# A decoder layer's feed-forward: first product as one plain product with resident weights, in place of seven half-size products with streamed sums

## The chip, the cores and the metric

The kernel runs on one core of a Trainium2 chip. The metric is the device time of one execution in microseconds (us); lower is better. Engines are named as in the profile: PE is TensorE, DVE is VectorE, ACT is ScalarE, POOL is GpSimd, SP is SyncE, which only issues transfers here.

## What is computed

One post-norm decoder layer on x of shape (8, 512, 512) in float32: relative-position self-attention, cross-attention to a context (8, 512, 1024), and a feed-forward block, each followed by a residual sum and a layer norm. The change is in the feed-forward block alone, cut here to what matters:

```python
h = jax.nn.relu(jnp.einsum('bsd,hd->bsh', x, w1) + b1)   # w1: (2048, 512)
hq = float_quantize(h, 4, 3)
out = jnp.einsum('bsh,dh->bsd', hq, wq) + bq             # wq = quantized w2
x = _layernorm(x + float_quantize(out, 5, 10))
```

## The kernel before

There are two phases. The first (lines 190 to 618) computes self-attention for all rows and projects the context to keys and values; it keeps both in DRAM. It ends at about 1,000 us of the profiled span. The change does not touch its source.

The second phase (from line 631) goes over eight blocks t of 512 rows. In stage t the kernel does the attention of block t (`scores`, `attend`) and, woven between these steps, the dense work of the blocks before it: the output projection of block t-1 (`project_x1`, `project_u`), its norm (`normalize_x2`), the transposed reload of the result (`load_x2T`, `turn_x2`), the queries of block t+1 (`load_x1T`, `turn_x1`, `queries`), the hidden layer of block t-1, and `finish` of block t-2, which is the second feed-forward product in FP8, the residual and the last norm.

The order of PE, DVE, ACT and SP is written by hand. `dense` is a list of steps with a cost each, `attention` a second list; `weave` (line 1174) takes from the one or the other by these costs. `run` (line 676) adds 0.7 of a step's cost to a credit, and pays from it small pieces of DVE and ACT work that wait in the queues `side` and `urgent` (softmax pieces, norms, stores). So a step's cost sets the order in which instructions stand, and nothing else. Each engine then runs its own instructions in that order and waits on semaphores.

The hidden layer (line 991, `hidden_steps`) multiplies w1 (2048 x 512) by the block transposed, `x2T` (512 x 512). It splits both in two halves each way and uses seven products of half size in place of eight (the Winograd form of Strassen's scheme). Each of eight rounds n makes hidden rows n and n+8 (of 16 chunks of 128) from fourteen matmuls, each 128x128 by 128x256. Each float32 matmul stands as two instructions in the profile, so a round is 28 rows of 128x256. The seven left operands, four of them sums of w1's blocks, stand in a ring of three slots (`ring`). In stage t=1, POOL builds them (`load_w1`, `sums_of_a`) from w1 as it arrives in 128 KB pieces, and SP stores each slot to DRAM (`w1d`); in all later stages ACT's queue reloads a slot for each round, 896 KB each. The right operands are four quarters of `x2T` and three sums of them, built by DVE after the turn (`sums_of_x2`, line 742). Partial results go from PSUM through ACT copies and DVE adds (lines 1015, 1021, 1035, 1041, 1045, 1054) to the ReLU on ACT (line 1048), which writes `hq` in FP8. All of it shares four PSUM banks (`bank`, line 649) with the other dense steps.

In the last stretch, after block 7's attention, nothing is left to weave; there the code cuts `finish` of block 6, rows 2 and 3, into quarters, and places one in each round.

Two further places matter. Line 727 turns a block of 512 x 512 on DVE in four instructions after a transposed load. Line 857 moves each head pair's attention weights between partitions (`pT<-pb`, sixteen SP transfers of 128 KB) before `attend` can use them.

Of the kernel before, what the change touches and what calls it, by code (L numbers as in the profile page):

```python
# [13 lines left out]
ALU = mybir.AluOpType  # L14
# [28 lines left out]
def decoder_layer(  # L43
# [46 lines left out]
    w1d = [dram.tile([P, 7, 2, P], F32, name=f"w1d{n}") for n in range(HC // 2)]  # L90
# [540 lines left out]
    with ExitStack() as ph:  # L631
# [110 lines left out]
        def sums_of_x2(t):  # L742
            b = [
                x2T[t][:, 2 * i : 2 * i + 2, k * W : (k + 1) * W]
                for i in range(2)
                for k in range(2)
            ]
            sums_of_b(nc.vector, *b, *(tx[:, i] for i in range(3)))

        def turn_x2(t):  # L750
            for c in range(EC):
                turn_in_place(x2T[t], c)
            sums_of_x2(t)
# [202 lines left out]

        W = S // 2
        HH2 = HC // 2
        RING = 3

        def turn_last_x2(j):
            t = T - 1
            if j == 0:
                settle(("x2", t))
                x2T[t] = qx.tile([P, EC, S], F32, tag="x2T", name=f"x2T{t}")  # L970
            turn(x2T[t], x1[t], j, f"x2tr{t}")
            if j == NJ - 1:
                sums_of_x2(t)

        def load_w1(m):

            n = m % HH2
            w = ring[:, m % RING]
            if m >= HH2:
                nc.scalar.dma_start(w, w1d[n])  # L980
                return
            lo, hi = slice(n * P, (n + 1) * P), slice((n + HH2) * P, (n + HH2 + 1) * P)
            w1c = chunked(w1T)
            nc.sync.dma_start(w[:, A11], w1c[:, 0:2, lo])
            nc.sync.dma_start(w[:, A12], w1c[:, 2:4, lo])
            nc.sync.dma_start(w[:, S3], w1c[:, 0:2, hi])
            nc.sync.dma_start(w[:, A22], w1c[:, 2:4, hi])
            sums_of_a(nc.gpsimd, w)
            later.append([3, lambda: nc.sync.dma_start(w1d[n], w)])

        def hidden_steps(t):


            x, y, z, tm2 = {}, {}, {}, {}

            def product(ps, n, a, b, start):


                for e in range(2):
                    nc.tensor.matmul(  # L1000
                        ps[:, 0:W],
                        lhsT=ring[:, (t * HH2 + n) % RING, a, e, :],
                        rhs=b[:, e, :],
                        start=start and e == 0,
                        stop=e == 1,
                        skip_group_check=not start,
                    )

            def b(i, k):
                return x2T[t][:, 2 * i : 2 * i + 2, k * W : (k + 1) * W]  # L1010

            def p2(n):
                y[n] = bank(f"hy{t}_{n}")
                product(y[n], n, A12, b(1, 0), True)
                nc.scalar.copy(tmp[:, n % 2, 0:W], y[n][:, 0:W])

            def p5(n):
                z[n] = bank(f"hz{t}_{n}")
                product(z[n], n, S1, tx[:, 0], True)
                tm2[n] = sm.tile([P, W], F32, tag="tm2", bufs=2, name=f"tm2_{t}_{n}")  # L1020
                nc.scalar.copy(tm2[n], z[n][:, 0:W])

            def begin():

                tag, bufs = ("qT", 2) if t == T - 1 else ("hq", 1)
                hq[t] = qx.tile([P, HC, S], F8, tag=tag, bufs=bufs, name=f"hq{t}")
                p5(0)
                p2(0)

            def p13(n):  # L1030
                x[n] = bank(f"hx{t}_{n}")
                product(x[n], n, A11, b(0, 0), True)
                product(z[n], n, S4, b(1, 1), False)
                c11 = tmp[:, n % 2, 0:W]
                nc.vector.tensor_tensor(c11, x[n][:, 0:W], c11, ALU.add)  # L1035

            def p6(n):
                if t * HH2 + n + 2 < T * HH2:
                    load_w1(t * HH2 + n + 2)
                product(x[n], n, S2, tx[:, 1], False)  # L1040
                nc.scalar.copy(tmp[:, n % 2, W:S], x[n][:, 0:W])  # L1041
                if n + 1 < HH2:
                    p2(n + 1)
                c12 = tmp[:, n % 2, W:S]
                nc.vector.tensor_tensor(c12, z[n][:, 0:W], c12, ALU.add)

            def relu(n, qs, src):
                nc.scalar.activation(
                    hq[t][:, n, qs], src, AF.Relu, bias=col(C_B1 + n), saturate=False
                )  # L1050

            def p7(n):
                product(x[n], n, S3, b(0, 1), False)
                nc.vector.tensor_tensor(tm2[n], x[n][:, 0:W], tm2[n], ALU.add)  # L1054
                if n + 1 < HH2:
                    p5(n + 1)
                relu(n, slice(0, S), tmp[:, n % 2])

            def p4(n):
                product(x[n], n, A22, tx[:, 2], False)  # L1060
                relu(n + HH2, slice(0, W), x[n][:, 0:W])
                relu(n + HH2, slice(W, S), tm2[n])

            steps = of(1.7, begin)
            for n in range(HH2):
                steps += of(1.7, p13, n) + of(1.7, p6, n) + of(1.7, p7, n)
                steps += [(0.9, True, lambda n=n: p4(n))]
            return steps

        def finish(t, j, n, part=0, parts=1, block=None):  # L1070

            if j % n == 0 and part == 0:
                mvc[t] = sm.tile([P, n, 2], F32, tag="mv", name=f"mvc{t}_{j}")
            if part == 0:
                o_bank[j] = block or bank(f"o{t}_{j}")
            po = o_bank[j]
            for c in range(HC * part // parts, HC * (part + 1) // parts):
# [7 lines left out]
            if part < parts - 1:  # L1085
                return
# [22 lines left out]
        o_bank = {}  # L1109
# [36 lines left out]
        ring = tx = tmp = None  # L1146

        def take_ring():

            nonlocal ring, tx, tmp  # L1150
            ffn = big.tile([P, FC * 2 * E], F32, tag="big", name="ffn")
            at = 0

            def part(*shape):
                nonlocal at
                n = math.prod(shape)
                names = "abcd"[: len(shape)]
                w = ffn[:, at : at + n].rearrange(
                    f"p ({' '.join(names)}) -> p {' '.join(names)}",
                    **dict(zip(names, shape)),  # L1160
                )
                at += n
                return w

            ring = part(RING, 7, 2, P)
            tx = part(3, 2, W)
            tmp = part(2, S)
            load_w1(0)
            load_w1(1)

        def of(cost, f, *a):
            return [(cost, False, lambda: f(*a))]

        def weave(dense, attention):

            dense, attention = list(dense), list(attention)
            left = sum(c for c, _, _ in dense)  # L1180
            weights = sum(w for _, _, _, w in attention)
            nd, gap = 0, 2.0
            while dense or attention:
                ready = attention and (not dense or attention[0][1] <= nd)
                if ready and (not dense or gap <= 0.0 or (dense[0][1] and gap < 1.5)):
# [3 lines left out]
                else:  # L1189
                    cost, _, step = dense.pop(0)  # L1190
# [31 lines left out]
        def output_of(t):  # L1222
# [3 lines left out]
            for j in range(NJ - 1):  # L1226
                steps += of(2.7, project_x1, t, j)
            steps += of(3.8, attend_next, t, EC - 1)
            for j in range(NJ - 1):
                steps += of(2.7, project_u, t, j)  # L1230
            last = NJ - 1
            return steps + of(2.7, project_x1, t, last) + of(2.7, project_u, t, last)

        ET = mybir.EngineType
        with tc.manual_schedule(engines={ET.PE, ET.DVE, ET.Activation, ET.SP}):
# [11 lines left out]
            for t in range(T):  # L1247
# [3 lines left out]
                asked = [of(3.5, queries, t + 1, o, mq) for o in range(EC) if t + 1 < T]  # L1251
                asked = sum(asked, [])
                if t == 0:
# [25 lines left out]
                    for piece in pieces[:-2]:  # L1279
                        dense += of(6.9, piece)  # L1280
# [12 lines left out]
                else:  # L1293
                    done = [of(3.5, finish, t - 2, j, NJ) for j in range(NJ) if t > 1]
                    if t == 1:

                        done = [of(6.9, pieces[-2]), of(6.9, pieces[-1]), [], []]
# [7 lines left out]
                    if t == 1:  # L1305
                        dense += of(0.0, take_ring)
                    dense += done[2] + done[3]
                    if t + 1 < T:
                        dense += of(0.0, turn_x1, t + 1)
                    dense += asked[:2] + of(0.0, turn_x2, t - 1) + asked[2:]  # L1310
                    queried = len(dense)
                    hidden = hidden_steps(t - 1)
                    hidden[HC:HC] = of(0.0, load_x1, t)
                    dense += hidden
                weave(dense, attention_of(t, projected, queried))

            last = of(3.5, finish, T - 2, 0, NJ) + output_of(T - 1)
            last += of(0.0, normalize_x2, T - 1)
            last += of(3.5, finish, T - 2, 1, NJ)
            for j in range(NJ):  # L1320
                last += of(0.6, turn_last_x2, j)

            gaps = []
            for j in (2, 3):

                def quarter(j, i):
                    block = ps_s.tile([P, 2, S], F32, tag="s", name=f"ol{j}")[
                        :, 0
# [102 lines left out]
```

## Time and profile before

| What | Value |
|---|---|
| Median of 3 runs | 2190.15 us (2187.91 to 2191.26) |
| The profiled execution's own time | 2196.65 us |
| Its span (first to last instruction) | 2194.5 us |
| Mean granted PE clock | 0.978 of full |
| PE busy | 2055.4 us, 94% of the span |
| DVE busy | 1567.5 us, 71% |
| ACT busy | 553.3 us, 25% |
| POOL busy | 170.7 us, 8% |
| Bytes moved by DMA | 316.35 MB, mean 144 GB/s |

A matmul row shows a busy time with a modelled end: one 128x512 float32 row reads 592 ns, but the next one starts 429 ns after it. So the rate of a stream is read from the starts of neighbouring rows, and a busy share of 94% still hides small waits. In the rows of the view in order of time, the bracket at the end tells how long the engine sat idle before the row, and what released it.

### The profile page before, as it was taken

The page shows a single profiled execution, that of the slowest core. Times are in us where ns is not written, and L with a number is a line of the kernel's source. Part 1 is how long each engine was busy: PE and PEld are TensorE (multiplying, and loading weights), DVE is VectorE, ACT ScalarE, POOL GpSimd, SP SyncE. Part 2 cuts the span into 40 slices and gives each one's busy share as a digit, 9 for nine tenths or more (in the row PEclk, how much of TensorE's full clock was granted, in tenths as well). Part 3 has the DMA queues.
Part 4 walks back from the last instruction along what each step waited for, and adds up shares of the span by engine and source line. Part 5 has one row for each costly group of instructions (what it writes and reads, how often), then busy time and mean ns, then how long its engine had stood idle before and what let it go on. Part 6 is the DMA issues. An engine that isn't in the chain of part 4 may idle for free.

```text
span 2194.5 us, 21443 instructions
## 1 busy us (share of the span) xinstructions
PE 2055.4 (94%) x7312; PEld 1186.9 (54%) x7312; DVE 1567.5 (71%) x2602; ACT 553.3 (25%) x1267; POOL 170.7 (8%) x156
## 2 busy tenths in 40 slices
PE   7999999999989999988997999999999999998898
PEld 5564665466447576733344446365464553644555
DVE  3799998999989998255664586665856767657434
ACT  2011101110201111122233335243352332524322
POOL 1000110011001001100013101001000010100000
PEclk9999999999999999999998999999999999999999
DMA  8130443035124235884486777676675757656612
GB/s 291 58 130 10 144 168 125 17 129 179 55 96 135 77 111 174 273 230 124 104 176 187 176 152 218 110 202 160 133 225 114 175 170 136 204 125 156 180 51 89
DMA packets 269117, 316.35 MB, mean 144 GB/s; under 512 B 142929, under 2 KB 171601, under 8 KB 269009
## 3 DMA queue, kind: packets, MB, share of 16 engines
q1 hardware_dynamic: 244720, 234.99, 41.4%
q10 hardware_dynamic: 24288, 80.00, 11.2%
q8 instruction: 58, 0.95, 0.2%
q14 instruction: 51, 0.41, 0.1%
HBM read 181.22 MB, written 66.58 MB: 113 GB/s over the span
## 4 chain that ended last, share of the span: by engine, by line
PE 58%; DVE 26%; DMA 8%; SPq 3%; issue 2%; ACT 2%; POOL 0%; ACTq 0%; DVEq 0%; POOLq 0%
PE hx L1000 9%; PE px L540 7%; PE pox L925 5%; PE pox L913 5%; PE hz L1000 4%; PE s L792 4%; PE pz L540 4%; DVE pv L429 4%; PE av L891 4%; PE ps_q L339 3%; DVE pb L844 2%; PE po L455 2%; SPq L857 2%; PE hy L1000 2%; DVE pv L439 2%
## 5 line engine op out<-in xcount | busy, mean ns | idle before, releaser
L817 ACT ACTIVATE pe<-pe,nmax 128x512 f32<-128x512 f32 x256 | 182.2, 713 | 245.6 <-DVE nmax L807 243.7
L807 DVE CUSTOM_DVE_ANT_0 pe<-s,mb 128x512 f32<-128x512 f32 x256 | 164.2, 682 | 56.0 <-PE s L792 54.8
L844 DVE STREAM_TRANSPOSE pb<-pe 128x512 f32<-128x512 f32 x256 | 161.0, 680 | 0.7 <-issue 0.2
L429 DVE TENSOR_TENSOR pv<-v,sc 128x2048 f32<-128x2048 f32 x64 | 148.5, 2321 | 2.0
L380 DVE TENSOR_TENSOR pq<-qw,k 128x2048 f32<-128x2048 f32 x64 | 147.2, 2300 | 1.1
L1000 PE MATMUL hx<-ffn 128*128 128x256 f32 x512 | 134.9, 386 | 13.2 <-DVE ffn L1035 6.6
L389 DVE TENSOR_REDUCE sc<-pq 128x64 f32<-128x2048 f32 x64 | 146.1, 2282 | 1.4
L1000 PE MATMUL hx<-x2T,ffn 128*128 128x256 f32 x512 | 138.2, 393 | 8.9 <-ACT ffn L1041 5.0
L891 PE MATMUL av<-pT,vx 128*64 128x512 f32 x512 | 124.8, 632 | 14.3 <-DMA pT<-pb 14.3
L772 PE MATMUL psq<-x1Ts,w_tgt 128*128 128x512 f32 x256 | 122.0, 632 | 16.5 <-DVE x1Ts L727 16.5
L832 DVE TENSOR_SCALAR pe<-pe,rden 128x512 f32<-128x512 f32 x256 | 132.6, 560 | 4.5
L792 PE MATMUL s<-kT,qTx 64*128 64x512 f32 x512 | 128.2, 617 | 3.4 <-DVE nmax L807 3.2
L1000 PEld LDWEIGHTS hx<-x2T,ffn 128*128 128x128 f32 x512 | 94.8, 192 | 52.3 <-issue 27.9
L455 PE MATMUL po<-w_o,aoT 128*128 128x512 f32 x256 | 117.1, 600 | 0.7 <-ACT aoT L452 0.7
L339 PE MATMUL ps_q<-w_in,xt 128*128 128x512 f32 x256 | 116.8, 594 | 0.3 <-DVE qw L366 0.3
L925 PE MATMUL pox<-w_xo,uT 128*128 128x512 f32 x256 | 115.2, 598 | 0.0
L1000 PEld LDWEIGHTS hx<-ffn 128*128 128x128 f32 x512 | 91.5, 190 | 42.5 <-DVE tm L1054 11.8
L913 PE MATMUL pox<-w_xo,x1Ts 128*128 128x512 f32 x256 | 114.4, 595 | 0.0
L339 PE MATMUL ps_k<-w_in,xt 128*128 128x512 f32 x256 | 114.0, 593 | 0.0
L932 DVE TENSOR_TENSOR x<-pox,x 128x512 f32<-128x512 f32 x32 | 22.1, 692 | 126.7 <-PE pox L925 79.2
L339 PE MATMUL ps_v<-w_in,xt 128*128 128x512 f32 x256 | 111.6, 594 | 0.0
L1078 PE MATMUL o<-w2q,hq 128*128 128x512 fp8e4 x480 | 106.1, 379 | 0.0
(179 smaller groups left out, 3114.6 us busy)
## 6 DMA issues: line engine op xcount, KB each, us to landing
pT<-pb SPq DMA_DIRECT2D x512, 128.0 KB, 2.4
ffn<-w1d ACTq DMA_DIRECT2D x56, 896.0 KB, 6.3
ch<-in_ctxT_dram SPq DMA_DIRECT2D x56, 256.0 KB, 3.3
td<-tx SPq DMA_DIRECT2D x28, 384.0 KB, 3.2
tx<-td SPq DMA_DIRECT2D x28, 384.0 KB, 5.6
r<-in_x_dram SPq DMA_DIRECT2D x32, 256.0 KB, 3.7
xt<-in_xT_dram SPq DMA_DIRECT2D x32, 256.0 KB, 2.6
x1d<-r ACTq DMA_DIRECT2D x32, 256.0 KB, 3.6
```

The lines of the kernel that those rows point to most:

```text
L339: nc.tensor.matmul(ps, lhsT=xt[:, e, :], rhs=w_in[:, e, part * E : (part + 1) * E], start=(e == 0), stop=(e == EC - 1),)
L429: nc.vector.tensor_tensor(pr, v_all[:, :, fs].rearrange("p s (h d) -> p s h d", d=D1), sc[:, t, g * HH * T : (g + 1) * HH * T] .rearrange( ...
L455: nc.tensor.matmul(po, lhsT=aoT[:, c * P : (c + 1) * P], rhs=w_o[:, c, :], start=(c == 0), stop=(c == EC - 1),)
L540: nc.tensor.matmul(bank[:, first], lhsT=w7[:, a, f, ps] if part == 0 else b[f][:, ps], rhs=b[f] if part == 0 else w7[:, a, f, :], start=st ...
L792: nc.tensor.matmul(ps[:, h, :], lhsT=qT[t][half[h], c, j * P : (j + 1) * P], rhs=kT[t, c][half[h], :], start=True, stop=True,)
L807: nc.vector.tensor_tensor_reduce(out=pe, in0=ps[:, h, :], in1=mb[t], scale=1.0, scalar=FMAX, op0=ALU.add, op1=ALU.min, accum_out=nmax[:, h ...
L817: nc.scalar.activation(pe, pe, AF.Exp, bias=nmax[:, h : h + 1], scale=-1.0, accum_out=den[:, h : h + 1],)
L844: nc.vector.transpose(pb[t, c][:, :, jj, :, h, i, :].rearrange("p a k e -> p k a e"), prs[2 * i + h].rearrange("p (k a e) -> p k a e", a=4 ...
L891: nc.tensor.matmul(av[half[h], :], lhsT=v[t, c][:, s, half[h]], rhs=pT[t, c][:, :, :, s, h].rearrange("p g i q -> p (g i) q"), start=(s == 0),
L913: nc.tensor.matmul(po, lhsT=x1T[t][:, e, j * P : (j + 1) * P], rhs=w_xo[:, e, :], start=(e == 0), stop=False,)
L925: nc.tensor.matmul(po, lhsT=uT[t][:, e, j * P : (j + 1) * P], rhs=w_xo[:, EC + e, :], start=False, stop=(e == EC - 1),)
L1000: nc.tensor.matmul(ps[:, 0:W], lhsT=ring[:, (t * HH2 + n) % RING, a, e, :], rhs=b[:, e, :], start=start and e == 0, stop=e == 1, skip_grou ...
```

## The change

`hidden_steps`, the ring, the sums and the temporaries go. `load_w1` brings the whole of w1 (4 MB, 32 KB per partition) into the same buffer of the pool `big` in four SP transfers of 1 MB, once, in stage t=1. `hidden(t, n)` makes one chunk of 128 hidden rows with four matmuls of 128x128 by 128x512 into one bank, and one ReLU on ACT. The step costs of the weaving change, `turn_x1` of the next block stands one `finish` step earlier, and the last stretch has no quarters of `finish` any more: `finish` of block 6, rows 1 and 2, stands ahead of the turns of block 7, and row 3 behind them.

```diff
-        def sums_of_x2(t):
...
         def turn_x2(t):
             for c in range(EC):
                 turn_in_place(x2T[t], c)
-            sums_of_x2(t)
...
+        w1 = []
+
+        def load_w1():
+
+            w1.append(big.tile([P, EC, HID], F32, tag="big", name="w1"))
+            for q in range(4):
+                qs = slice(q * E, (q + 1) * E)
+                nc.sync.dma_start(w1[0][:, :, qs], chunked(w1T)[:, :, qs])
+
+        def hidden(t, n):
+
+            if n == 0:
 
                 tag, bufs = ("qT", 2) if t == T - 1 else ("hq", 1)
                 hq[t] = qx.tile([P, HC, S], F8, tag=tag, bufs=bufs, name=f"hq{t}")
...
+            ps = bank(f"h{t}_{n}")
+            for e in range(EC):
+                nc.tensor.matmul(
+                    ps,
+                    lhsT=w1[0][:, e, n * P : (n + 1) * P],
+                    rhs=x2T[t][:, e, :],
+                    start=(e == 0),
+                    stop=(e == EC - 1),
+                )
+            nc.scalar.activation(
+                hq[t][:, n, :], ps, AF.Relu, bias=col(C_B1 + n), saturate=False
+            )
...
-                if ready and (not dense or gap <= 0.0 or (dense[0][1] and gap < 1.5)):
+                if ready and (not dense or gap <= 0.0):
...
-                steps += of(2.7, project_x1, t, j)
+                steps += of(3.6, project_x1, t, j)
...
-                steps += of(2.7, project_u, t, j)
+                steps += of(3.6, project_u, t, j)
...
-                    dense += done[2] + done[3]
+                        dense += of(0.0, load_w1)
+                    dense += done[2]
                     if t + 1 < T:
                         dense += of(0.0, turn_x1, t + 1)
+                    dense += done[3]
                     dense += asked[:2] + of(0.0, turn_x2, t - 1) + asked[2:]
                     queried = len(dense)
-                    hidden = hidden_steps(t - 1)
-                    hidden[HC:HC] = of(0.0, load_x1, t)
-                    dense += hidden
+                    for n in range(HC):
+                        dense += of(3.6, hidden, t - 1, n)
+                        if n == HC // 4:
+                            dense += of(0.0, load_x1, t)
...
-            last = of(3.5, finish, T - 2, 0, NJ) + output_of(T - 1)
+            last = of(3.8, finish, T - 2, 0, NJ) + output_of(T - 1)
             last += of(0.0, normalize_x2, T - 1)
-            last += of(3.5, finish, T - 2, 1, NJ)
+            for j in (1, 2):
+                last += of(3.8, finish, T - 2, j, NJ)
             for j in range(NJ):
                 last += of(0.6, turn_last_x2, j)
...
-            for cost, gap, step in hidden_steps(T - 1):
-                if gap:
-                    last += [gaps.pop(0)]
-                last += [(cost, gap, step)]
+            last += of(3.8, finish, T - 2, 3, NJ)
+            for n in range(HC):
+                last += of(3.6, hidden, T - 1, n)
             for j in range(NJ):
-                last += of(3.5, finish, T - 1, j, 1)
+                last += of(3.8, finish, T - 1, j, 1)
```

## Prediction, made before the changed kernel ran

> **What bounds the kernel now.** I read the page's busy shares first, then PE's rows in order of time, then the waits on PE and SP.
>
> ```profile
> PE 2055.4 (94%) x7312; PEld 1186.9 (54%) x7312; DVE 1567.5 (71%) x2602; ACT 553.3 (25%) x1267; POOL 170.7 (8%) x156
> ...
> L1000 PE MATMUL hx<-ffn 128*128 128x256 f32 x512 | 134.9, 386 | 13.2 <-DVE ffn L1035 6.6
> ```
>
> PE is the bound, but 386 ns for a half-width row against 592 for a full one has modelled ends. The starts give the rate:
>
> ```profile
> 1471.03 1.03 PE L1000 MATMUL hy<-x2T,ffn 128*128 128x256 f32 x4
> 1471.90 1.03 PE L1000 MATMUL hx<-x2T,ffn 128*128 128x256 f32 x4
> ...
> 1477.08 1.03 PE L1000 MATMUL hy<-x2T,ffn 128*128 128x256 f32 x4
> ```
>
> From one `hy` to the next is a round of 28 rows: 6.05 us, 0.216 a row. A full-width row takes 0.429 (chain of waits: `pox` L913, 8 rows in 3.43). So PE streams without a gap here, and the seven products do save time at full stream. What remains are gaps. I list them as lost time: a group's next start, less its own start, less its rows times their pitch (0.216, 0.429; scores 0.24, `av` 0.224). The largest:
>
> ```profile
> 1133.71 2.07 PE L1000 MATMUL hx<-x2T,ffn 128*128 128x256 f32 x4 [3.84 <-DVE qTx L779]
> ...
> 1179.65 2.08 PE L1000 MATMUL hy<-x2T,ffn 128*128 128x256 f32 x4 [11.61 <-DMA ffn<-in_w1T_dram]
> ...
> 1189.28 1.13 PE L1000 MATMUL hy<-x2T,ffn 128*128 128x256 f32 x4 [1.41 <-DMA ffn<-in_w1T_dram]
> ...
> 1200.11 1.60 PE L1000 MATMUL hy<-x2T,ffn 128*128 128x256 f32 x4 [2.41 <-DMA ffn<-in_w1T_dram]
> ```
>
> This is stage t=1, where the ring is built: the hidden stretch lasts 95.3 us (1127.9 to 1223.2), in t=3 the same work takes 67.7. After a long gap four rows take 2.07 instead of 1.03: the granted clock of this stretch is 0.87, elsewhere 1.00.
>
> ```profile
> 1421.55 8.83 PE L772 MATMUL psq<-x1Ts,w_tgt 128*128 128x512 f32 x16 [2.23 <-DVE x1Ts L727]
> ...
> 1443.92 1.13 PE L1000 MATMUL hx<-ffn 128*128 128x256 f32 x4 [1.10 <-DVE ffn L1035]
> ...
> 1504.14 1.13 PE L1000 MATMUL hx<-x2T,ffn 128*128 128x256 f32 x4 [0.46 <-ACT ffn L1041]
> 1505.92 1.13 PE L1000 MATMUL hx<-ffn 128*128 128x256 f32 x4 [0.65 <-DVE tm L1054]
> ...
> 1998.87 2.07 PE L1000 MATMUL hz<-ffn 128*128 128x256 f32 x4 [6.73 <-DVE ffn L143]
> ...
> 2007.56 1.13 PE L1000 MATMUL hx<-x2T,ffn 128*128 128x256 f32 x4 [1.34 <-ACT ffn L1041]
> ...
> 2048.80 6.20 PE L891 MATMUL av<-pT,vx 128*64 128x512 f32 x16 [4.68 <-DMA pT<-pb]
> ```
>
> The first four recur in every stage; the last three are in t=7. SP's waits explain the last one:
>
> ```profile
> SPq L857 <- DMA ffn<-w1d: 89.9, 13, 11.8
> ```
>
> Transfers take eight completion semaphores in turn, so a `pT` transfer can wait for a ring load that ACT has not issued yet. In t=7 that wait reaches PE.
>
> Lost time by stage:
>
> - hidden of t=1: 30.8;
> - the products' own waits on their sums (L1035, L1041, L1054), t=2 to 6: 16.7;
> - queries waiting for the turn L727, t=2 to 6, with the slow clock after three of them: 17.3;
> - t=7: 18.6;
> - the last stretch, from 2108: 4.4.
>
> Together 87.8 us.
>
> **The change, part by part.** *The products.* Per round 28 rows at 0.216 go (6.05) and 16 rows at 0.429 come (6.86): +0.81. There are 8 rounds in 8 blocks, so **+52 us**, all on PE's path. The switch to and from woven steps costs about 0.1 in both forms.
>
> *The sums.* DVE loses 24 adds of 0.42 and four sums of about 0.69 per block, ACT three copies of 0.37 per round, POOL its 25 us. Their busy time counts nothing, as PE covers them; only the waits listed go. ACT's ReLU becomes 16 of 0.73 per block, 11.6, in place of 22.5 for copies and ReLUs. It is hidden as long as ACT lags by less than three products (10.3 us), since four banks are there. So **-16.7** in t=2 to 6.
>
> *The weights.* The built program has four `w1` transfers on SP where the first ring loads stood, right after the `x2T` load, and none later. SP issued there at 1119.8; `x2T` landed at 1124.5. A 1 MB transfer of the same row length (`w2f`) lands in 5.5 to 8.1 us: the first quarter is there between 1125.3 and 1127.9, when PE finishes the queries (1127.5). Two loads of 2 MB (`w_src`) land within 14.2 us: all by about 1134 to 1139. Behind it on SP stand `vx` and the sixteen `pT` of the next `attend`, paced by the same semaphores: ten more issues of 0.6 after 1138 and 2.4 to land give 1146 to 1147; PE reaches that `av` at 1127.9 + 4 x 3.43 + 1.9 = 1143.5. I expect 2 to 3 lost there, with 2 of slow clock: 5 left of 30.8, **-25.8**. The wait for `qTx` goes as well, because the four sums (2.8, stretched to 4.0 there) stood before it on DVE, and the plain form needs that bank 6.9 later. Bounds: nothing left; or 14 left, by the slowest 1 MB load (`w_in`, 12.4: 4.3 lost, 5.0 of slow clock as at 1133.7) and a late `pT` (5).
>
> *The turn of x1* moves ahead of the last `finish`. Counting from the first `finish` product, in the new order PE reaches the queries at 19.2 (four products of 3.43, scores 1.92, `av` 3.58). DVE's queue before the turn ends at 17.7: from 3.7, when product one is out, a chain of 2.3, three norms (1.6 with their reciprocal), waiting to 9.0 for product two, its chain 2.3, a norm 0.5, three softmax pieces 1.85, the chain of product three 2.3, a piece 0.7, a division 1.04. The first turned quarter is 0.73 later, 18.4. The slack is 0.8, so I take 2.5 left of 17.3: **-14.8**. Bounds: 0 to 17.3 left. What is late next is PE itself.
>
> *Stage t=7.* The reload of `x2T` stays late (DVE waited for it until 1995.75), but the products can begin on the first turned quarter instead of after all four and a sum: at 1996.5 instead of 1998.9. About 4.4 and 1.5 of slow clock stay. With no ring loads, `pT` waits only for SP's own. 6 left of 18.6, **-12.6**; bounds 1 to 13 left.
>
> *The last stretch.* Two `finish` products now cover the norm (1.87 of waiting), one covers the last ACT copy and the sums go: 1 left of 4.4, **-3.4**, bounds 0 to 4.4. The quarters' work only moves.
>
> *Before t=1* a scores step moves ahead of one query product. That scores step was waiting for DVE already; the wait grows by up to 3.4, and two later waits (2.2, 2.8) shrink. I take 0, bounds -2.5 to +2.5.
>
> Sum: 52 - 25.8 - 16.7 - 14.8 - 12.6 - 3.4 = **-21 us**. The profiled execution took 2196.65 (span 2194.5, 2.2 around it); it becomes 2175.4. The median of the runs, 2190.15, is 6.5 below it; the same change gives **2169 us**.
>
> [...] In t=3, 5 and 6 the queries ran slow after gaps of only 2.2 us: 8.83 against 7.13, 1.9 lost each. [...]
>
> **The rivals.**
>
> *The gaps stay where they were (little or nothing).* If the turn still ends late (slack 0.8 against DVE pieces of 0.7 each), 14.8 come back; if the 4 MB hold up the first product and `pT` to about 11, 6 come back. 52 - 87.8 + 36 = 0: about **2190**. For it: both margins are small. Against: the turn stands a whole product earlier, and `w1` comes in one stream.
>
> *Banks become the bound (slower).* The plain form holds a full bank per product. Place: the first products after the queries, which need the banks that `qTx` empties, behind softmax pieces on DVE. Price as measured at 1133.7: 4.0 lost, 5 more with the slow clock. If it recurs in t=2 to 7: 24 to 54 more, +3 to +33, middle **2208**. It decides from 3.5 us per stage. For it: DVE is 71% busy and takes its queue in order. Against: DVE loses 13 us a stage, and in my walk `qTx` ends 7 us before the bank is needed; in t=2 to 7 no row waits 3 us for `qTx`.
>
> *All gaps go.* Nothing is left anywhere: 52 - 87.8 = -36, **2154**.
>
> *It doesn't do what it says.* The built program shows 4 loads and 128 products of four matmuls; no chance for that.
>
> **How the numbers follow.** Forecast 2169 (2157 to 2182): 0.64. Gaps stay (2182 to 2196): 0.16. Banks (2193 to 2223): 0.13. All gaps go (below 2157): 0.07. The range, 2154 to 2200, leaves out most of the banks' case. Faster or slower by over 0.2% means below 2185.8 or above 2194.5, about what a measurement of this kernel can tell from no change: faster 0.64 + 0.07 + a third of the second case = 0.77; slower 0.12, same 0.11.
>
> **What would show it.** Right: 128 groups of eight rows at 3.43 without brackets; the stretch of t=1 near 75 us instead of 95.3; queries following `finish` directly; no bracket at the second `av` of t=7; stages t=2 to 6 as long as before (141 to 144 us). Wrong: brackets before `h` that name `qTx` or the ReLU, `av` waiting for `pT` in each stage, or a pitch above 0.43 for `h`.

## The result and the profile after

| | Before | After |
|---|---|---|
| Median of 4 runs | 2189.03 us (2185.73 to 2191.26) | 2162.76 us (2161.87 to 2164.02) |
| Ratio | | 0.9882, 95% interval 0.9865 to 0.9899 |
| Profiled execution: own time, span | 2196.65, 2194.5 us | 2161.87, 2160.1 us |
| Mean granted PE clock | 0.978 | 0.989 |
| Bytes moved by DMA | 316.35 MB | 257.48 MB |

The kernel became faster by 1.2%, 26.3 us between the medians; the forecast had been 21 us less, 2169. Lines of the second phase stand earlier in the new file: the hidden product is L970, its ReLU L977, the turn L726, the queries L762, `finish` L987, the load of w1 L960.

The page of the profile after, first the busy shares, then the chain that ended last by engine, then two groups (busy time, mean ns of one, idle time just before):

```profile
PE 2080.1 (96%) x6544; PEld 1040.1 (48%) x6544; DVE 1453.5 (67%) x2378; ACT 479.8 (22%) x1011; POOL 143.7 (7%) x124
...
PE 75%; DVE 16%; DMA 5%; issue 1%; SPq 1%; ACT 1%; POOL 0%; ACTq 0%; DVEq 0%
...
L970 PE MATMUL h<-x2T,w 128*128 128x512 f32 x1024 | 454.7, 599 | 4.5 <-DVE x2T L726 4.5
...
L977 ACT ACTIVATE hq<-h,colv 128x512 fp8e4<-128x512 f32 x128 | 88.0, 687 | 302.4 <-PE h L970 302.4
```

PE is busy for longer than before (2080.1 against 2055.4 us) in a shorter span: it does more work and waits less. PE's share of the chain that ended last was 58% before and is 75% now. All 1024 rows of the new product waited 4.5 us together. The 302.4 us are ACT waiting for PE; no row of PE waits for the ReLU, so the four banks never stood in its way.

The start of the hidden product in t=1, PE in order of time (start, busy, engine, line, rows, bracket for idle time and its releaser):

```profile
1117.40 7.13 PE L762 MATMUL psq<-x1Ts,w_tgt 128*128 128x512 f32 x16
1124.37 7.03 PE L970 MATMUL h<-x2T,w 128*128 128x512 f32 x16
1131.33 1.99 PE L782 MATMUL s<-kT,qTx 64*128 64x512 f32 x8
1133.25 7.13 PE L970 MATMUL h<-x2T,w 128*128 128x512 f32 x16
1140.32 3.65 PE L881 MATMUL av<-pT,vx 128*64 128x512 f32 x16
...
1152.88 14.00 PE L970 MATMUL h<-x2T,w 128*128 128x512 f32 x32
```

No row has a bracket. The weights were there when the queries ended, and so was `pT` when PE came to `av` at 1140.32, but only just: the last of its sixteen transfers, issued at 1136.63, landed 3.5 us later, some 0.1 to 0.2 us ahead of PE. The whole stretch runs from 1124.37 to 1195.33, 71.0 us, where the same block took 95.3.

The change of work in the next stage, PE again, and the first turn piece of that stage from DVE's rows:

```profile
1246.87 3.63 PE L987 MATMUL o<-w2q,hq 128*128 128x512 fp8e4 x16
1250.34 3.60 PE L762 MATMUL psq<-x1Ts,w_tgt 128*128 128x512 f32 x8
...
1392.15 3.60 PE L762 MATMUL psq<-x1Ts,w_tgt 128*128 128x512 f32 x8
```

```profile
1248.34 2.48 DVE L726 STREAM_TRANSPOSE x1Ts<-x1Ts 128x512 f32<-128x512 f32 x4
```

The queries follow `finish` directly. DVE began the turn 2.0 us before PE needed its first quarter. A stage lasts 1392.15 - 1250.34 = 141.81 us, and the next three are equal to it to 0.01 us: PE waits no longer in one of them than in another.

What is left is the start of the hidden product in t=7:

```profile
1959.48 1.99 PE L782 MATMUL s<-kT,qTx 64*128 64x512 f32 x8
1965.93 13.44 PE L970 MATMUL h<-x2T,w 128*128 128x512 f32 x24 [4.47 <-DVE x2T L726]
1979.31 1.99 PE L782 MATMUL s<-kT,qTx 64*128 64x512 f32 x8
```

PE waits 4.47 us for the reloaded `x2T`. Then 24 rows take 13.38 us from start to start, where 24 times 0.429 is 10.3: 3.08 us of slow clock (the granted clock was 0.50 from 1964.93 to 1971.76).

### The profile page after: what moved, and what is told of

Its sections match the earlier page's. It is cut to its first block, busy times and chain, and to the rows that moved or that the text cites. A ratio compares the mean times of both kernels' runs of the same rounds, so it can differ in the third digit from the quotient of the medians.

```text
span 2160.1 us, 19078 instructions
## 1 busy us (share of the span) xinstructions
PE 2080.1 (96%) x6544; PEld 1040.1 (48%) x6544; DVE 1453.5 (67%) x2378; ACT 479.8 (22%) x1011; POOL 143.7 (7%) x124
## 2 busy tenths in 40 slices
DMA packets 253297, 257.48 MB, mean 119 GB/s; under 512 B 141456, under 2 KB 161936, under 8 KB 253200
## 4 chain that ended last, share of the span: by engine, by line
PE 75%; DVE 16%; DMA 5%; issue 1%; SPq 1%; ACT 1%; POOL 0%; ACTq 0%; DVEq 0%
PE h L970 21%; PE px L539 7%; PE pox L915 5%; PE av L881 5%; PE s L782 5%; PE pox L903 5%; PE psq L762 4%; PE o L987 4%; DVE pv L428 4%; PE pz L539 4%; PE ps_q L338 3%; PE po L454 2%; DVE pv L438 2%; DVE sc L388 2%; DVE pq L379 2%; PE py L539 2%
## 5 line engine op out<-in xcount | busy, mean ns | idle before, releaser
L970 PE MATMUL h<-x2T,w 128*128 128x512 f32 x1024 | 454.7, 599 | 4.5 <-DVE x2T L726 4.5
L970 PEld LDWEIGHTS h<-x2T,w 128*128 128x128 f32 x1024 | 192.2, 191 | 263.4 <-issue 253.9
L977 ACT ACTIVATE hq<-h,colv 128x512 fp8e4<-128x512 f32 x128 | 88.0, 687 | 302.4 <-PE h L970 302.4
L881 PE MATMUL av<-pT,vx 128*64 128x512 f32 x512 | 119.2, 608 | 8.9 <-DMA pT<-pb 8.9
L762 PE MATMUL psq<-x1Ts,w_tgt 128*128 128x512 f32 x256 | 117.0, 610 | 5.8 <-DVE x1Ts L726 5.8
L822 DVE TENSOR_SCALAR pe<-pe,rden 128x512 f32<-128x512 f32 x256 | 116.9, 499 | 4.5
L987 PE MATMUL o<-w2q,hq 128*128 128x512 fp8e4 x512 | 114.1, 379 | 0.0
L900 POOL TENSOR_TENSOR x<-x,bxo 128x512 f32<-128x512 f32 x32 | 39.9, 1279 | 817.7 <-DMA x<-x1d 318.6
```

What stands on the lines that cost most here:

```text
L762: nc.tensor.matmul(ps, lhsT=w_tgt[:, e, o * P : (o + 1) * P], rhs=x1T[t][:, e, :], start=(e == 0), stop=(e == EC - 1),)
L881: nc.tensor.matmul(av[half[h], :], lhsT=v[t, c][:, s, half[h]], rhs=pT[t, c][:, :, :, s, h].rearrange("p g i q -> p (g i) q"), start=(s == 0),
L970: nc.tensor.matmul(ps, lhsT=w1[0][:, e, n * P : (n + 1) * P], rhs=x2T[t][:, e, :], start=(e == 0), stop=(e == EC - 1),)
L987: nc.tensor.matmul(po, lhsT=hq[t][:, c, j * P : (j + 1) * P], rhs=w2q[:, c, :], start=(c == 0), stop=(c == HC - 1),)
```

## The experiments

Times are medians; ratios are against runs of the kernel before on the same chip (medians 2187.25 to 2188.88 us). The experiments ran on several chips, so where two of them are compared, the ratios are the better measure. My theory was the prediction's: the seven products save 52 us of PE's rows and lose 88 in waits that each have a cause of their own. The rivals: the fewer bytes are what helps; half-width rows cost more than their pitch says; waits only move elsewhere.

### The turn of x1, moved alone

```diff
-                    dense += done[2] + done[3]
+                    dense += done[2]
                     if t + 1 < T:
                         dense += of(0.0, turn_x1, t + 1)
+                    dense += done[3]
```

> The kernel before with one edit: the turn of the next block's x1 stands one finish product earlier, as in the changed kernel. Theory (the gain is the sum of removed gaps, each with its own cause and price, and the products themselves cost 52 us more): the five waits of the queries for the turn go, 13 to 17 us less, about 2173, and no bracket that names the turn is left in t=2 to 6. Rival 1 (the gain is relief of the DMA queues from the streamed sums): 0 to 3 us less. Rival 2 (half-width rows cost more than their pitch shows): 0 to 3 us less.

Measured: 2176.01 us, ratio 0.9945 (0.9926 to 0.9963): 12.0 us less, 8 to 16 by the interval. Stage t=2, PE:

```profile
1265.30 3.65 PE L891 MATMUL av<-pT,vx 128*64 128x512 f32 x16
1268.89 7.13 PE L772 MATMUL psq<-x1Ts,w_tgt 128*128 128x512 f32 x16
...
1290.21 1.13 PE L1000 MATMUL hx<-ffn 128*128 128x256 f32 x4 [1.49 <-DVE ffn L1035]
```

All five waits for the turn are gone. A part came back: the wait of the first round on its sum (L1035) grew from 1.10 to 1.49 us, and with it the loss there from 1.27 to 1.77, 2.5 in five stages. By the rows 14.8 of the 17.3 remain as a gain, and the measured 12 holds that within its interval.

### The same move undone in the new kernel

The edit is the reverse of the one above, in the kernel after.

> The changed kernel with the turn of x1 put back behind the last finish product. Theory: the wait returns, and longer than before, since the last finish product now stands right before the queries: about 4 us in each of t=2 to 6 and 2 to 4 of slow clock, 20 to 40 us more, about 2190. Rivals 1 and 2: 0 to 5 us more.

Measured: 2184.37 us, ratio 0.9981 (0.9967 to 0.9994): 21.6 us slower than after.

```profile
1251.13 5.40 PE L762 MATMUL psq<-x1Ts,w_tgt 128*128 128x512 f32 x8 [3.16 <-DVE x1Ts L726]
...
1398.07 5.40 PE L762 MATMUL psq<-x1Ts,w_tgt 128*128 128x512 f32 x8 [3.17 <-DVE x1Ts L726]
...
1838.87 5.40 PE L762 MATMUL psq<-x1Ts,w_tgt 128*128 128x512 f32 x8 [3.16 <-DVE x1Ts L726]
```

The wait is there in all five stages, 3.16 us, and the eight rows behind it run slow, 1.9 more each time (5.33 from start to start against 3.43; the mean granted clock of this execution is 0.986, after's 0.989). The stage grows from 141.81 to 146.94, 25.6 us in five; the time before the second phase was 3.4 shorter in this profile (936.5 against 939.9), and the rest, 22, is what was measured. By the rows, the wait is longer than the 2.2 us of the kernel before because there an `av` of 3.58 us stands between the last `finish` and the queries on PE and covers part of DVE's work ahead of the turn; here nothing stands between, and DVE's 2.3 us on that `finish` (1248.02 to 1250.36) and the first quarter of the turn lie open. So plain products and resident weights without the moved step would have been worth 4 us under the kernel before (1 to 7 by the interval).

### No reloads of the ring

The kernel before, without the 56 transfers that reload the ring from t=2 on; it leaves out these loads, so the products of blocks 1 to 7 use whatever the ring holds.

```diff
             if m >= HH2:
-                nc.scalar.dma_start(w, w1d[n])
                 return
```

> The kernel before without the 56 reloads of the ring on ACT's queue (50 MB). It leaves out those loads: later rounds multiply with whatever weights the ring still holds. Theory: only the late attention transfer of t=7 reached PE, so 7 to 9 us less, about 2181; the build of the sums in t=1, the own waits and the turn stay. Rival 1: most of the gain, 20 us less or more. Rival 2: 0.

Measured: 2177.61 us, ratio 0.9953 (0.9935 to 0.9971): 10 us less. The second `av` of t=7, which had waited 4.68 us and run slow:

```profile
2032.93 3.65 PE L891 MATMUL av<-pT,vx 128*64 128x512 f32 x16
```

The wait for `pT` is gone. All the other waits are still there: 11.43 us in t=1's build, 2.29 for the turn in every stage, 5.86 for `x2T` in t=7. So the rival that fewer bytes are what helps (20 us or more) is out: a sixth of all bytes went (264.95 MB are left of 316.35) and only one wait with them. In before, SP stood 89.9 us before `pT` transfers until a ring load had come, 13 times; only in t=7 did PE then wait for `pT`. In that trace all 1039 transfers of SP and 158 of ACT use the same eight completion semaphores, in 987 of 1196 steps the next one in turn, and none was issued before the one ahead of it on its semaphore had landed. `pT` transfers also landed late beside the loads: one issued at 2032.67 in before, just behind a ring load, took 6.95 us to land, and the 137 issued while a ring load was in flight took 6.9 in the median, the other 375 2.4. This experiment takes away both at once.

### Half-width rows

The new kernel with each 128x512 product made as two of 128x256 into the halves of the same bank.

```diff
-                nc.tensor.matmul(
-                    ps,
...
+                for k in range(2):
+                    ks = slice(k * E // 2, (k + 1) * E // 2)
+                    nc.tensor.matmul(
+                        ps[:, ks],
...
+                        rhs=x2T[t][:, e, ks],
```

> The changed kernel with each product of 128x512 cut into two of 128x256 with the same weights: 2048 half-width rows and as many weight loads instead of 1024. Theory: 16 rows of 0.2158 against 8 of 0.429 are 0.02 us per chunk, 2 to 4 us more in all, about 2166. Rival 2: 20 us more or beyond. Rival 1: 0.

Measured: 2164.83 us, ratio 0.9885 (0.9866 to 0.9904), 2.1 us above after's median and 0.7 by the ratios, which the intervals don't tell from nothing. Stage t=1, PE:

```profile
1125.11 7.07 PE L972 MATMUL h<-x2T,w 128*128 128x256 f32 x32
1132.11 1.99 PE L782 MATMUL s<-kT,qTx 64*128 64x512 f32 x8
```

32 half-width rows take 7.00 us from start to start, as 16 whole ones do (6.96). Half-width rows cost half. The old products lost by their waits, not by their shape.

### Taking the build out of t=1

The rest asks whether the seven products could have been kept. First all eight slots of sums are built and stored in the first phase, and t=1 only loads them.

```diff
+        def build_w1():
+            w1c = chunked(w1T)
+            for n in range(HC // 2):
...
+                w = wa.tile([P, 7, 2, P], F32, tag="w1b", name=f"w1b{n}")
...
+                sums_of_a(nc.gpsimd, w)
+                nc.sync.dma_start(w1d[n], w)
+
         for part in range(2):
+            if part == 1:
+                build_w1()
...
-            if m >= HH2:
-                nc.scalar.dma_start(w, w1d[n])
-                return
...
+            nc.scalar.dma_start(w, w1d[n])
```

> The kernel before, with its seven half-size products, but with all 56 slots of weight sums written out during the first phase, so that t=1 no longer builds sums by the row and only loads them like t=2 to t=7. My theory: the 30.8 us that t=1 lost waiting for the build go almost wholly, 25 to 29 us under the kernel before, and the stages t=2 to t=6 keep their waits for the turn of x1 and their own small waits. Rival, the build of t=1 was only in the way of waits that come next in the same stage: 15 us under or less. Rival, the first phase becomes longer by what GpSimd, SP and the loads do in it: no gain, or a loss of up to 20 us.

> As e5_prebuilt, with the turn of x1 moved up by one finish as well. My theory, in which the seven products save 52 us of TensorE's rows and give most of it back in waits that can be taken away one at a time: 36 to 42 us under the kernel before, so some 10 to 15 us under the kernel after, with the own small waits of each stage and the pT wait of t=7 still there. Rival, the waits only move elsewhere when two of them are taken away: no faster than the kernel after.

Measured: 2191.44 us, ratio 1.0016 (1.0003 to 1.0028), and with the turn moved 2175.85, 0.9948 (0.9933 to 0.9962). My theory fell, by the second rival. The hidden stretch of t=1 is as short as hoped, 72.7 us (1144.99 to 1217.70, behind a wait of 5.05 us for a sum of `x2T`) against 95.3, but the first phase became some 15 to 20 us longer: the second phase's first dense row (`psk`, L161) begins at 959.0 us (953.4 with the turn moved), where it was 943.2 in before and 936.5 to 938.7 in the four runs above, whose first phase is the same program. PE early in the first phase, then SP's waits from 60 to 160 us (total, times, longest):

```profile
134.59 1.22 PE L553 MATMUL py<-ch,w 128*128 128x256 f32 x2 [11.96 <-DMA ch<-in_ctxT_dram]
...
147.43 1.22 PE L553 MATMUL py<-ch,w 128*128 128x256 f32 x2 [5.38 <-DMA ch<-in_ctxT_dram]
```

```profile
SPq L534 <- POOL w1b L140: 29.3, 7, 5.1
SPq L532 <- DMA w1d<-w1b: 19.6, 7, 3.5
SPq L534 <- DMA w1b<-in_w1T_dram: 14.4, 12, 2.1
```

In SP's order of issue each store (L534) stands before the next loads (L532), and the context loads stand behind both. The stores waited 29.3 us for POOL's sums in this stretch, the loads 19.6 until a store had landed.

Next, one slot with each of eight contexts, each stored one context later:

```diff
+        def build_w1(n):
+            if n:
+                nc.sync.dma_start(w1d[n - 1], w1b[n - 1])
...
                 lo, hi, tx = context_of(t, part)
+                if part * (T - 1) + t <= HC // 2:
+                    build_w1(part * (T - 1) + t)
```

> As e5_prebuilt, but the eight slots of weight sums are built one at a time, one with each of the first eight contexts of the first phase, each stored only with the next context, so that SP never stands before a store whose sums GpSimd has not finished. In e5_prebuilt TensorE waited 12.0 and 5.4 us for context loads at 134.6 and 147.4 us, and the first phase ended some 20 us later than in the other runs of the same program. My theory: that was SP's wait, so the first phase is as long as before again, and what t=1 gained stays: 20 to 27 us under the kernel before, 22 being nearest to what e5_prebuilt showed in t=1. Rival, the loads of the prebuilt slots or GpSimd's sums themselves cost the first phase what they take, wherever they stand: 0 to 8 us under.

> As e7_spread, with the turn of x1 moved up by one finish. My theory: the two gains add, 32 to 40 us under the kernel before, so 6 to 14 us under the kernel after, at some 2150 us; the small own waits of each stage and the pT wait of t=7 are still there. Rival, what is taken away in one place comes back in the next: not faster than the kernel after.

Measured: 2193.99 us, ratio 1.0026 (1.0009 to 1.0044), and 2181.57, 0.9968 (0.9952 to 0.9983). This says nothing of spreading, because it was not spread: the order of the first phase is a scheduler's, and it drew all eight builds forward: their loads stand at 51.8 to 147.0 us, their last store at 160.4, and the first `psk` row comes at 962.4. PE waited 12.43 and 6.63 us for `ch` at the same place.

So the third form gives the scheduler a reason: POOL copies a column of a context's keys into the slot before the loads, and stores from its own queue.

```diff
+            for a in (A11, A12, S3, A22):
+                nc.gpsimd.tensor_copy(w[:, a, 0, 0:1], late[:, 0:1])
...
-                nc.sync.dma_start(w1d[n - 1], w1b[n - 1])
+            nc.gpsimd.dma_start(w1d[n], w)
...
+                if 0 < part * (T - 1) + t <= HC // 2:
+                    build_w1(part * (T - 1) + t - 1, st[0])
```

> As e7_spread, but each slot's loads are tied to the keys of one context by a small copy that GpSimd makes from them into the slot, so that the scheduler can't draw all eight builds to the front (in e7_spread it did: SP stood 64.9 us before loads and stores of the slots between 60 and 160 us, and TensorE waited 12.4 and 6.6 us for context loads there), and each slot is stored from GpSimd's own queue. My theory: the first phase is within 5 us of that of the kernel before, and what t=1 gains (some 22 us in e5_prebuilt) stays: 17 to 25 us under the kernel before. Rival, the sums and loads themselves cost the first phase what t=1 gains: 0 to 8 us under.

> As e9_tied, with the turn of x1 moved up by one finish. My theory: the gains of e9_tied and of e1_turn_early add: 28 to 37 us under the kernel before, so as fast as the kernel after or up to 10 us under it. Rival, the gains don't add, and the kernel after stays ahead by 5 us or more.

Measured: 2182.16 us, ratio 0.9965 (0.9951 to 0.9979), and 2170.76, 0.9914 (0.9896 to 0.9931). The builds are spread now (from 245 to 732 us), and the long waits at 134 us are gone; yet the first `psk` row still comes 8 to 15 us late, at 951.2. My theory (within 5 us) fell here too. PE's waits in the first 943 us, without the reloads (whose first phase is before's) and with the tied builds:

```profile
PE aot L450 <- DVE ao L445: 13.1, 11, 2.8
PE py L540 <- DMA ch<-in_ctxT_dram: 8.6, 4, 4.3
```

```profile
PE aot L450 <- DVE ao L445: 17.3, 12, 5.2
PE py L552 <- DMA ch<-in_ctxT_dram: 14.3, 7, 5.2
```

PE waits 10 us more for these two. The `ao` group of DVE takes 495 ns apiece here and 467 without the builds. So the rival holds, with 7.7 us under before where it said 0 to 8: the first phase has little room for POOL's sums and their loads, at either place that was tried. Which of the two costs it the time was not separated. The two gains did add, though (by their ratios 12.0 and 7.7 us under before alone, 18.8 together), so waits do not simply move on. The kernel after stays ahead by 7 us by the ratios (8 between the medians).

### A mixture

Here block 0 alone is plain. w1 is loaded whole in t=1 as in the kernel after, hidden rows n and n+8 are made in pairs, and POOL makes the sums in place behind each pair and stores them; t=2 to t=7 and the end use the seven products, with the turn moved. The second form reloads the ring from POOL's queue in place of ACT's.

```diff
             lo, hi = slice(n * P, (n + 1) * P), slice((n + HH2) * P, (n + HH2 + 1) * P)
...
+            a11, a12 = w1[0][:, 0:2, lo], w1[0][:, 2:4, lo]
+            a21, a22 = w1[0][:, 0:2, hi], w1[0][:, 2:4, hi]
...
+            nc.gpsimd.tensor_tensor(a22, a21, a22, ALU.add)
+            nc.gpsimd.tensor_tensor(a21, a11, a21, ALU.subtract)
+            nc.gpsimd.tensor_tensor(a11, a22, a11, ALU.subtract)
+            nc.gpsimd.tensor_tensor(a12, a12, a11, ALU.subtract)
```

```diff
-            nc.scalar.dma_start(ring[:, m % RING], w1d[m % HH2])
+            nc.gpsimd.dma_start(ring[:, m % RING], w1d[m % HH2])
```

> The seven products with the turn of x1 moved up (as e1_turn_early), except that block 0 takes the plain form: in t=1 the whole of w1 is loaded in four transfers as in the kernel after, hidden rows n and n+8 are made in pairs, and GpSimd makes the sums in place behind each pair and stores them from its own queue, so that t=2 to t=7 reload slots as before. Neither t=1 nor the first phase has a build in the way. My theory, in which the stages t=2 to t=6 of e1_turn_early are 2.3 us shorter than those of the kernel after (139.5 against 141.8), t=1 is like after's and t=7 and the end are like before's: 24 us under e1_turn_early, some 35 under the kernel before, so 2150 to 2156, 7 to 13 under the kernel after. Rival, the stores and sums disturb t=1 or the first reloads: no faster than the kernel after (2163).

> As e11_hybrid, but the ring is reloaded from GpSimd's queue, so that these transfers no longer share completion semaphores in turn with SP's. My theory: the pT wait of t=7 goes as in e2_no_reload, 5 to 8 us under e11_hybrid. Rival, GpSimd issues the reloads late, because its own waits stand before them: slower than e11_hybrid, with brackets in every stage that name the ring.

Measured: the mixture 2157.51 us, ratio 0.9853 (0.9833 to 0.9874); with POOL's reloads 2167.55, 0.9907 (0.9889 to 0.9926). The mixture's median is 5 us under the kernel after (6 by the ratios), but the two intervals overlap (0.9865 to 0.9899 for after), so that it beats it is likely and not shown. It is 18.5 us under the first experiment (20 by the ratios), where 24 were expected. PE in the mixture:

```profile
1136.79 3.65 PE L892 MATMUL av<-pT,vx 128*64 128x512 f32 x16 [3.02 <-DMA kT<-kd]
...
1266.78 1.13 PE L1043 MATMUL hx<-x2T,ffn 128*128 128x256 f32 x4 [2.13 <-DVE qTx L780]
...
1391.83 7.13 PE L773 MATMUL psq<-x1Ts,w_tgt 128*128 128x512 f32 x16
...
1531.51 7.13 PE L773 MATMUL psq<-x1Ts,w_tgt 128*128 128x512 f32 x16
```

The middle stages take 139.68 us, 2.1 less than after's 141.81, as expected. Two new waits cost more than what is missing. In t=1 `av` waited 3.02 us; the bracket names the load of `kT`, which this product does not read, but SP issued its sixteen `pT` transfers from 1116.47 on and the last at about 1132.4; with 4.2 us to land, the median of after from 1110 to 1145, that one came at 1136.6, just before `av` began. By this estimate it was `pT` that came late. At the start of t=2's products the wait for `qTx` and what follows it cost 6.9 us in four groups, where the later stages lose 1.8 there.

In the second form the middle stages got longer (141.5 to 142.6 us for t=3 to t=5, against 139.7 to 139.9), by waits like these:

```profile
1449.33 1.13 PE L1043 MATMUL hy<-x2T,ffn 128*128 128x256 f32 x4 [1.05 <-DMA ffn<-w1d]
...
1465.86 1.13 PE L1043 MATMUL hx<-ffn 128*128 128x256 f32 x4 [1.73 <-DVE tm L1097]
```

The products now wait for the ring, and the wait on a sum is 1.73 where the mixture has 0.50. As for the shared semaphores: in the mixture SP still stood before `pT` transfers for ring loads,

```profile
SPq L858 <- DMA ffn<-w1d: 66.8, 13, 7.8
```

and with the reloads on POOL's queue SP's waits hold no such line. That part of the theory holds. But `av` in t=7 still waited 3.07 us for `pT` (4.70 in the mixture). By this comparison the shared semaphores made up 1.6 us of the wait, though the reloads also stand at other times in the two. That the rest is transfers landing late beside a ring load is my estimate from before, where these took 6.9 us in the median against 2.4. The late ring cost more than was gained: the rival is right.

## Why the prediction was right

Lost time as in the prediction, before and after, against the terms of its sum (us):

| Term | Predicted | Before | After | Measured |
|---|---|---|---|---|
| products | +52 | 1792 rows x 0.2158 | 1024 x 0.429 | +52.6 |
| build in t=1 | -25.8 | 30.8 | 0 | -30.8 |
| the products' own waits | -16.7 | 16.7 | 0 | -16.7 |
| turn of x1 | -14.8 | 17.3 | 0 | -17.3 |
| t=7 | -12.6 | 18.6 | 7.6 | -11.0 |
| last stretch | -3.4 | 4.4 | 0 | -4.4 |
| sum | -21 | | | -27.6 |

The spans differ by 34.4 us. The first phase, which the change does not touch, gives 3.3 of it (taken up to the first `psk` row, 943.2 before, 939.9 after): the profiled execution of before was a long one, as its own time, 7.6 above the median of its runs, also says. Of the other 31.1 the table has 27.6. Most of the rest lies in gaps of under 0.25 us, which the prediction did not list: in the rows from the first hidden product to the last `finish` they add up to 10.3 us before and 6.6 after, by the same pitches. They are reckoned against pitches over some thousand rows, so these two sums are good to a few us only. All of this is one execution of each kernel; the 26.3 us between the medians are the better size of the gain.

- *The products, +52.* Right. The half-width rows test confirms that both forms run at their pitch, so the plain form really costs PE more. In the five middle stages, with the turn moved in both, the seven products are the faster form: 139.0 to 139.9 us per stage in the first experiment against 141.81.
- *The weights in t=1.* The mechanism was right, the size was off: nothing is left, where I took 5. I had put the issue of w1 at 1119.8; SP issued it at 1114.7. Of these 5.1 us 3.5 are the whole stage, which came earlier, and 1.6 are SP's. The four transfers took 7.2 to 12.4 us to land, and the first was there when PE came at 1124.4. The sixteen `pT` were issued by 1137.2, not 1144, and PE did not wait at 1140.3. That nothing at all is left was luck: the last `pT` landed 0.1 to 0.2 us before PE came, and in the mixture, with two of the four loads in another order and POOL's stores beside them, the same `av` waited 3.02, by the estimate above for it.
- *The turn.* Right in kind: the new order is worth 21.6 in the new kernel. I took 2.5 left; nothing is, because DVE got to the turn 2.0 us ahead of PE, not 1.5 (0.73 of each is the first quarter's own time). Slack of 0.8 was reckoned, 1.3 was there. It is not one price for both kernels: alone in the old one it was worth 12, and undone in the new one it costs 25.6 by the stages, since the wait is 3.16 there, not 2.23, and in the profiled execution the rows behind it run slow each time. The 17.3 hold 5.7 of slow clock, 1.9 in each of three stages; how many stages it hits depends on when the waits fall (see the last section), so the term would have been 11.6 with none and 21.1 with five. "Elsewhere 1.00" was a misreading of the granted clock: it was 0.50 for 3.4 us in each of these three stages, and 0.95 on the mean from 943 to 1127.9.
- *t=7.* The first products start on the first turned quarter as I said, and wait 4.47 where I had 4.4. The slow clock after it cost 3.08, not 1.5: that is the mis-sized term. The wait for `pT` is gone with the ring loads, and the run without reloads shows that these were its cause. The way was only half right: I put it on the semaphores taken in turn, but without sharing them 3.07 of the mixture's 4.70 remained, and in before `pT` transfers landed late beside a ring load (6.9 us in the median against 2.4).
- *The last stretch and the time before t=1.* No wait remains at the end (1 was taken). From the end of the first phase to the first hidden row it is 184.4 us after and 184.7 before: 0, as taken.
- *The slow clock after gaps of 2.2 us.* I counted it from the rows of three stages. That was right: the granted clock in the trace of before was 0.50 for 3.41 us at each of them, and the last section shows where these waits stood.
- *The rivals.* "Gaps stay" decided at slack 0.8 in the turn and on the arrival of w1: both held; with the turn put back the kernel is at 2184, near that rival's 2190. "Banks become the bound" needs waits for `qTx` or the ReLU before `h`: there is none. "All gaps go" (2154): 7.6 us of lost time are left of 87.8, so the result lies between this rival and the forecast.

That a kernel with 52.6 us more on PE is the faster one rests on the waits. By the runs, most of the 26 us needs the move of the turn: without it the new kernel is only 4 us under the old. The new step costs of the weaving were not tried by themselves.

## What to carry to other kernels

A scheme that saves multiplications must be charged with every wait that its sums, copies and streamed operands bring: here it saved 52 us of PE's rows and gave back 88, and the waits could be read one by one from the gaps between rows. When a change has several parts, cost and test the small ordering edits by themselves: moving one step past 3.4 us of cover was worth 22 us in the new kernel and 12 in the old. A build moved off the critical stage was not free where it landed (the first phase grew by 15 to 20 us, in the tied form by 8 to 15); look at what stands in order behind it on the queue that it uses, and whether a scheduler will leave it there.

## What the runs showed of the hardware

Short waits made PE's clock fall in some stages and not in others. After the same 2.2 to 2.3 us before the queries, 16 rows ran in 8.83 in three of five stages of the kernel before. In these two they ran in 7.13:

```profile
1280.58 7.13 PE L772 MATMUL psq<-x1Ts,w_tgt 128*128 128x512 f32 x16 [2.30 <-DVE x1Ts L727]
...
1564.18 7.13 PE L772 MATMUL psq<-x1Ts,w_tgt 128*128 128x512 f32 x16 [2.23 <-DVE x1Ts L727]
```

The granted clock in the traces of before and after shows what differed. In both it is either 1.00 or 0.50, and it changes only on a fixed grid: any two changes of a trace (33 in before, 19 in after) lie whole multiples of 3.413 us apart. In the kernel before, it was 0.50 from 1422.50 to 1425.91, one step of the grid, and the whole wait (1419.32 to 1421.55) lay in the step before that, from 1419.09 to 1422.50. So it was at 1705.80 and 1849.16. In the two fast stages an edge of the grid, at 1279.14 and 1562.45, cut the wait in two, and no step held more than 1.44 and 1.73 us of it. Over both traces, from the clock's first entry (36.7 and 39.8 us) on, a step at full clock with more than 2.0 us of idle PE (brackets over 0.1 us) was followed by half clock in 23 of 23 cases, one with less than 1.3 us never while PE still had rows to run, and between these both happened (half clock after 1.40 and 1.96, full clock after 1.87). So a step need not be idle as a whole: 2.2 us of 3.4 were enough here. Without the reloads too, after the same 2.29 us, 16 rows ran in 8.83 at 1272.03, 1414.83 and 1698.68 and in 7.13 at 1841.06. With the turn put back, where the wait is 3.16 us, the rows were slow in five of five: a stage of 146.94 us is 43.05 steps, so by this estimate the wait met the grid at nearly the same place each time. Three smaller points:

- The first `psk` row, up to which eight kernels have the same program, began at 936.5 to 943.2 us in their profiled executions. A term of a few us in a comparison of two profiles has to be read past that point.
- `pT` transfers of 128 KB landed late beside a ring load of 896 KB: in the kernel before the 137 that were issued while one was in flight took 6.9 us in the median, the other 375 took 2.4. There the two come from different queues, SP's and ACT's.
- POOL's 32 sums of 128x256 in the kernel before took 0.72 to 0.73 us in the median of each of the four lines, but up to 1.20, and DVE's `ao` group beside the tied builds took 6% longer (495 ns apiece against 467).
